# Where the third batch's router logits, its routing and its list entries stand in a gated mixture-of-experts block

## The chip, the core and the metric

The kernel runs on one core of a Trainium2 chip. The metric is the time of one execution in microseconds (us); the kernel before has a median of 522.15 us over 8 runs (516.1 to 529.22). All times on an engine's own clock below count from the start of the profiled span. PE is the matrix engine (PEld its weight loads), DVE the vector engine, ACT the engine for activations, POOL the general engine, SP the engine that here only issues transfers. DMA is the engines that move data.

## What is computed

Four batches of 512 tokens, 512 features each. An attention step adds a mix of features to each token; then a feed-forward step adds a shared expert and, for each token, its two best of eight experts:

```python
x = x + tanh(g_xattn[0]) * xattn(layernorm(x), ctx_1024, Wq, bq, Wk, bk)
x = x + tanh(g_ffn[0])   * ffn(layernorm(x), ...)

def ffn(x, ...):                                  # D = 512, H = 352, E = 8, TOP_K = 2
    shared_out = (silu(x @ Wg_s) * (x @ Wu_s)) @ Wd_s
    logits = x @ Wr + br + rb                     # 8 per token
    probs = sigmoid(logits)
    top_v, top_i = top_k(probs, 2)
    w = one_hot(top_i) * (top_v / sum(top_v))     # per token and expert
    routed_out = sum over e of swiglu(x, Wg[e], Wu[e], Wd[e]) * w[..., e]
    return shared_out + routed_out
```

All matrices are float32.

## The kernel before

**Stages.** B = 4 batches, NS = 4 tiles of 128 tokens in each. First come attention weights and attention output of the batches, with the shared expert's inner layer (`shared_hidden`) of batches 0 and 1 between them. Then, in code after the loop (lines 645 to 663), come the inner layers of batch 2 (`B - 2`, "the third") and batch 3 (`B - 1`, "the last"). After that come the shared expert's outer products of all 16 tiles (`shared_out`), with the search for what each block of the routed part must read between them, and then the routed part: 39 blocks of 128 tokens, each of one expert.

**Inner layer.** `shared_hidden(b, lo, hi, amid)` makes for each tile two products, `pg` (gate) and `pu` (up), each in four steps `c` over the features; `amid[c]` is called after step `c` and puts other small products there. ACT takes silu of `pg` (line 472), DVE multiplies by `pu` (line 475), and ACT's queue writes the tile to `hs_d` for regrouping.

**Logits.** The router's eight columns lie behind the up weights in `ws`. For a batch that isn't in `alone`, `pu` is 360 columns wide instead of 352 and its last eight are the logits (line 474 adds the bias). For a batch in `alone`, `logits(b, lo, hi)` makes them by themselves: for each tile four products of 128x8 (line 443), put amid an inner layer. In the kernel before, `alone` holds batches 2 and 3.

**Input of the inner layer.** The normalised rows of the last batch go to DRAM in quarters (`to_quarters`, POOL's queue, line 321), come back regrouped (`from_quarters`, SP's queue, line 327, `wbig<-xz_d`), and are turned by DVE (`turn`, line 331, `wbig<-wbig`). DVE works in the order of its queue: what stands behind a turn waits for that turn's transfer too.

**Routing.** `route(b)` is a chain of some 25 small DVE steps with one exponential on ACT, which needs another table there (line 497, then line 472's table again). It ends with a running count per expert: `pre` and `cum[b + 1]`, so that batch 3's follows batch 2's. `places(b)` makes two products on PE (line 520, `pl`: `tri` by `sel`, then `ones` by `pre`), from which DVE works out a place in the list for each token and choice (`place`, `ent`, lines 526 to 544). `scatter_places` issues eight scatters on POOL's queue for each batch (line 552, `slot_d<-ent,posi`), each of 128 entries. In the built program POOL's transfers share eight semaphores in turn, so each transfer on POOL's queue waits for the one that stands eight before it to have landed.

**List.** Line 700 (`ws<-slot_d`, POOL's queue) reads the finished list; it waits for all scatters. DVE copies it into another order (line 710, four copies), after the fifth outer product's addition by its place in the queue, and PE multiplies it by `pick` (line 642, `pq`) after the seventh of the 16 outer products (`po`, line 568). From `pq` come the indices of the gathers for the routed blocks.

**Buffers.** The small products and `pg`, `pu` share a pool of four PSUM buffers (`ps_mm`); a product that takes a buffer waits until its last reader is done.

Of the kernel before, what the change touches and what calls it, by code (L numbers as in the profile page):

```python
# [22 lines left out]
def flamingo_block(  # L23
# [17 lines left out]
    B, S, D = x.shape  # L41
# [96 lines left out]
    def after(later, earlier, reason="written before it is read"):  # L138
        tc.add_manual_dep(
            later.ins, earlier.ins.name,  # L140
            mybir.DependencyInfo(mybir.DependencyClass.Sync, mybir.DependencyReason.DATA),
            reason=reason,
        )
# [176 lines left out]
    def to_quarters(src, by, engine=nc.gpsimd):  # L320
        engine.dma_start(
            out=by.rearrange("(a p) w -> p a w", p=P), in_=src.rearrange("p (a w) -> p a w", a=NQ)
        )
# [98 lines left out]
    def normed_turned(b, lo, hi):  # L422
        def turns(behind):
            for s in range(lo, hi):
                t = turn(
                    xn_v[s].rearrange("p (b w) -> p b w", b=NQ), xnT_v[b % 2][:, :, ts(s, P)]
                )
                after(t, behind, "they come in meanwhile")

        return turns  # L430

    lg_b = {}
    alone = {B - 2, B - 1}
    scatters = []

    def logits(b, lo=0, hi=NS):

        if lo == 0:
            lg_b[b] = small.tile([P, NS, E], F32, tag="lg", name=f"lg_{b}")
        pr = ps_mm.tile([P, hi - lo, E], F32, tag="mm", name="pr")  # L440
        for s in range(lo, hi):
            for c in range(ND):
                p = nc.tensor.matmul(
                    pr[:, s - lo, :], lhsT=xnT_v[b % 2][:, c, ts(s, P)], rhs=ws[:, c, 2 * H :],
                    start=(c == 0), stop=(c == ND - 1),
                )
                after(p, product["last"], "not too many small ones at once")
        nc.vector.tensor_tensor(
            lg_b[b][:, lo:hi, :], pr,
            bias_r.rearrange("p (o e) -> p o e", o=1).broadcast_to([P, hi - lo, E]), ALU.add,  # L450
        )

    def shared_hidden(b, lo=0, hi=NS, amid={}):

        route_too = b not in alone
        if route_too and lo == 0:
            lg_b[b] = small.tile([P, NS, E], F32, tag="lg", name=f"lg_{b}")
        wide = HR if route_too else H
        for s in range(lo, hi):
            pg = ps_mm.tile([P, H], F32, tag="mm", name="pg")  # L460
            pu = ps_mm.tile([P, wide], F32, tag="mm", name="pu")
            for c in range(ND):
                for dst, at, n in ((pg, 0, H), (pu, H, wide)):
                    product["last"] = nc.tensor.matmul(  # L464
                        dst, lhsT=xnT_v[b % 2][:, c, ts(s, P)], rhs=ws[:, c, at : at + n],
                        start=(c == 0), stop=(c == ND - 1),
                    )
                if c in amid:
                    amid[c]()
            filled = h_sb[(b * NS + s) % OUT]  # L470
            h = filled[:, :H]
            nc.scalar.activation(h, pg, AF.Silu)
            if route_too:
                nc.vector.tensor_add(lg_b[b][:, s, :], pu[:, H:], bias_r)
            done = nc.vector.tensor_mul(h, h, pu[:, :H])
            at = (b * NS + s) * NQ * P
            to_quarters(filled, hs_d[at : at + NQ * P, :], nc.scalar)
        return done
# [12 lines left out]
    def route(b):  # L491

        lg = lg_b[b]

        nc.vector.tensor_scalar_max(lg, lg, -87.0)
        pr = small.tile([P, NS, E], F32, tag="pr", name=f"pr_{b}")
        nc.scalar.activation(pr, lg, AF.Exp, scale=-1.0)
        nc.vector.tensor_scalar_add(pr, pr, 1.0)
        nc.vector.reciprocal(pr, pr)
        at = [small.tile([P, NS, E], F32, tag=f"at{k}", name=f"at{k}_{b}") for k in range(TOP_K)]  # L500
        m1 = first_max(pr, b, at[0], 0)

        rest = small.tile([P, NS, E], F32, tag="rest", name=f"rest_{b}")
        nc.vector.scalar_tensor_tensor(rest, at[0], -4.0, pr, ALU.mult, ALU.add)
        m2 = first_max(rest, b, at[1], 1)

        sel = small.tile([P, NS, E], F32, tag="sel", name=f"sel_{b}")
        nc.vector.tensor_add(sel, at[0], at[1])
        pre = small.tile([P, NS, E], F32, tag="pre", name=f"pre_{b}")
        nc.vector.tensor_copy(pre[:, 0, :], cum[b])  # L510
        for s in range(NS):
            dst = pre[:, s + 1, :] if s + 1 < NS else cum[b + 1]
            nc.vector.tensor_add(dst, pre[:, s, :], sel[:, s, :])
        return at, m1, m2, sel, pre

    def places(b, at, m1, m2, sel, pre):

        pl = ps_mm.tile([P, NS * E], F32, tag="mm", name="pl")
        for i, (l, r) in enumerate(((tri, sel), (ones, pre))):
            p = nc.tensor.matmul(  # L520
                pl, lhsT=l, rhs=r.rearrange("p s e -> p (s e)"),
                start=(i == 0), stop=(i == 1),
            )
            after(p, product["last"], "the routing takes its time")
        place = small.tile([P, NS, E], F32, tag="place", name=f"place_{b}")
        nc.vector.tensor_add(place, pl.rearrange("p (s e) -> p s e", e=E), first)  # L526
        tot = small.tile([P, NS, 1], F32, tag="tot", name=f"tot_{b}")
        nc.vector.tensor_add(tot, m1, m2)
        nc.vector.reciprocal(tot, tot)
        nc.vector.tensor_scalar_mul(tot, tot, tgf)  # L530
        todo = []
        for k, m in enumerate((m1, m2)):
            nc.vector.tensor_mul(at[k], at[k], place)
            pos = small.tile([P, NS, 1], F32, tag=f"pos{k}", name=f"pos{k}_{b}")
            nc.vector.tensor_reduce(pos, at[k], AX.X, ALU.add)
            posi = small.tile([P, NS], I32, tag=f"posi{k}", name=f"posi{k}_{b}")
            nc.vector.tensor_copy(posi, pos.rearrange("p s o -> p (s o)"))
            low = small.tile([P, NS], I32, tag=f"low{k}", name=f"low{k}_{b}")
            nc.vector.tensor_single_scalar(low, posi, P - 1, op=ALU.bitwise_and)
            ent = small.tile([P, NS, 2], F32, tag=f"ent{k}", name=f"ent{k}_{b}")  # L540
            nc.vector.tensor_tensor(  # L541
                ent[:, :, 0], token[:, b * NS : (b + 1) * NS], low, ALU.subtract
            )
            nc.vector.tensor_mul(
                ent[:, :, 1], m.rearrange("p s o -> p (s o)"), tot.rearrange("p s o -> p (s o)")
            )
            todo += [(ent[:, s, :], posi[:, s : s + 1]) for s in range(NS)]
        return todo

    def scatter_places(todo, behind=None):  # L550
        for what, where in todo:
            sc = nc.gpsimd.indirect_dma_start(  # L552
                out=slot_d, in_=what,
                out_offset=bass.IndirectOffsetOnAxis(ap=where, axis=0),
                in_offset=None,
            )
            tc.declare_no_dep(sc.ins, group="places", reason="no two tokens share a place")
            tc.add_to_no_dep_group("places", sc.ins)
            after(sc, cleared)
            if behind is not None:  # L560
                after(sc, behind, "it delays less there")
            scatters.append(sc)
# [48 lines left out]
    routed = None  # L611
# [4 lines left out]
    for i in range(B):  # L616
# [12 lines left out]
        if i >= 2:  # L629
# [7 lines left out]
            routed = route(i - 2)  # L637
    power, _ = attention_out(B - 1, halves(B - 2))
    scatter_places(places(B - 3, *routed), power)
    def amid(dst, lhsT, rhs):  # L640
# [4 lines left out]
    routed = {}  # L645
    load_expert(4, None, (False, True))
    load_expert(5, None, (True, False))
    shared_hidden(B - 2, 0, 1, {1: lambda: logits(B - 2, 0, 2), 3: lambda: logits(B - 2, 2)})
    routed[B - 2] = route(B - 2)
    step = shared_hidden(B - 2, 1, 2)  # L650
    normed_turned(B - 1, 0, 2)(step)
    load_expert(5, step, (False, True))
    step = shared_hidden(
        B - 2, 2, 3, {1: lambda: scatter_places(places(B - 2, *routed[B - 2]))}
    )
    normed_turned(B - 1, 2, NS)(step)
    step = shared_hidden(
        B - 2, 3, NS, {1: lambda: logits(B - 1, 0, 2), 3: lambda: logits(B - 1, 2)}
    )
    routed[B - 1] = route(B - 1)  # L660
    load_expert(6, step)
    step = shared_hidden(B - 1, 0, 1)
    back_early(step)


# [19 lines left out]
    step = shared_hidden(B - 1, 2, 3, {1: count})  # L685
# [260 lines left out]
```

## Time and profile before

| what | value |
|---|---|
| median of 8 runs | 522.15 us (516.1 to 529.22) |
| profiled execution, time | 517.12 us |
| its span | 513.9 us, so 3.2 us lie around it |
| granted TensorE clock, mean | 0.992 |
| batch 2's inner layers on PE | 134.19 to 162.40 us |
| batch 3's inner layers on PE | 162.40 to 182.88 us |
| outer products, with `pq` and `pi` among them | 182.88 to 222.8 us |
| routed part on PE | 223.69 to 501.9 us |
| a pair of products of one step, `pg` and `pu` | 1.18 us (0.59 us each, start to start) |
| regrouped rows of batch 3: issue to landing | 7.1, 7.5, 6.6 and 9.7 us; issued 144.9 to 149.3 us |
| scatters: landing after issue | 7.3 to 17.3 us, median 10.7 |
| list read, line 700: landing after issue | 5.0 us |
| expert 7's gate and up weights | issued at 183.68 us, landing after 11.0 |

A row of the timeline gives start, duration, engine, line and operation, what is written from what is read, a count, and in brackets the idle time of the engine before it with what ended it. A merged row's duration reaches from its first start to its last end. float32 products are two passes in the trace, so `x2` is one product.

### The profile page before, as it was taken

The page shows a single profiled execution, that of the slowest core. Times are in us where ns is not written, and L with a number is a line of the kernel's source. Part 1 is how long each engine was busy: PE and PEld are TensorE (multiplying, and loading weights), DVE is VectorE, ACT ScalarE, POOL GpSimd, SP SyncE. Part 2 cuts the span into 40 slices and gives each one's busy share as a digit, 9 for nine tenths or more (in the row PEclk, how much of TensorE's full clock was granted, in tenths as well). Part 3 has the DMA queues.
Part 4 walks back from the last instruction along what each step waited for, and adds up shares of the span by engine and source line. Part 5 has one row for each costly group of instructions (what it writes and reads, how often), then busy time and mean ns, then how long its engine had stood idle before and what let it go on. Part 6 is the DMA issues. An engine that isn't in the chain of part 4 may idle for free. (4 is left out here: it accounts for less than half of the span.)

```text
span 513.9 us, 5436 instructions
## 1 busy us (share of the span) xinstructions
PE 493.8 (96%) x1507; PEld 275.2 (54%) x1507; DVE 231.5 (45%) x542; ACT 91.7 (18%) x163; POOL 265.4 (52%) x293
## 2 busy tenths in 40 slices
PE   8999999999999999999999999999999999999980
PEld 4444464465667644455555555555555555555540
DVE  1898965955856356553323322332233333322210
ACT  3355034112022000000111111111111111111110
POOL 3004230171265410545777777777477777777221
PEclk9999999999999999999999999999999999999996
DMA  6999994579998999724666656665555666666332
GB/s 196 395 366 370 340 337 136 163 176 143 314 239 120 215 179 322 219 82 129 123 140 121 124 121 135 124 127 117 122 108 137 128 124 134 123 127 127 55 44 38
DMA packets 67164, 87.86 MB, mean 171 GB/s; under 512 B 32992, under 2 KB 40032, under 8 KB 67136
## 3 DMA queue, kind: packets, MB, share of 16 engines
q1 hardware_dynamic: 43056, 55.08, 36.7%
q0 software_dynamic: 13184, 25.88, 26.8%
q10 hardware_dynamic: 10896, 6.56, 5.6%
q8 instruction: 14, 0.23, 0.2%
q14 instruction: 14, 0.11, 0.1%
HBM read 56.78 MB, written 30.70 MB: 170 GB/s over the span
## 5 line engine op out<-in xcount | busy, mean ns | idle before, releaser
L750 POOL DMA_INDIRECT x_all<-xz_d,idx x148 | 141.7, 957 | 79.8 <-issue 35.4
L331 DVE STREAM_TRANSPOSE x_all<-x_all 128x512 f32<-128x512 f32 (+1 forms) x71 | 69.9, 984 | 160.2 <-DMA x_all<-by 135.9
L785 PE MATMUL rg<-wbig,x_all 128*128 x296 | 111.9, 460 | 1.7 <-issue 0.9
L785 PE MATMUL ru<-wbig,x_all 128*128 x296 | 111.7, 459 | 0.0
L568 PE MATMUL po<-wbig,x_all 128*128 x222 | 101.4, 592 | 0.7 <-DVE x_all L836 0.7
L785 PEld LDWEIGHTS rg<-wbig,x_all 128*128 128x128 f32 x296 | 55.9, 190 | 43.1 <-issue 18.4
L813 POOL DMA_INDIRECT out_x<-ws,idx x37 | 59.6, 1611 | 31.8 <-issue 17.6
L785 PEld LDWEIGHTS ru<-wbig,x_all 128*128 128x128 f32 x296 | 56.2, 190 | 31.3
L568 PEld LDWEIGHTS po<-wbig,x_all 128*128 128x128 f32 x222 | 42.1, 190 | 44.0 <-issue 36.3
L398 PE MATMUL po<-wbig 128*128 128x512 f32 x128 | 56.4, 592 | 0.0
L464 PE MATMUL pu<-ws,wbig 128*128 128x360 f32 (+1 forms) x128 | 48.8, 463 | 1.4 <-DVE place L526 1.4
L464 PE MATMUL pg<-ws,wbig 128*128 128x352 f32 x128 | 49.3, 466 | 0.0
L793 ACT ACTIVATE h_all<-rg 128x352 f32<-128x352 f32 x37 | 17.2, 464 | 173.2 <-PE rg L785 173.2
L317 POOL TENSOR_TENSOR rstd<-ve,mhalf 128x4 f32<-128x4 f32 x8 | 8.2, 1024 | 71.9 <-DVE ve L315 38.5
L812 ACT ACTIVATE ws<-po,wts 128x512 f32<-128x512 f32 x37 | 25.4, 687 | 103.9 <-PE po L568 101.2
L568 PE MATMUL po<-wsd,wqk 128*128 128x512 f32 x96 | 42.5, 595 | 0.3 <-DVE wqk L331 0.3
L552 POOL DMA_INDIRECT slot_d<-ent,posi x32 | 31.1, 971 | 18.6 <-DVE ent L541 9.5
L398 PEld LDWEIGHTS po<-wbig 128*128 128x128 f32 x128 | 24.2, 190 | 29.4 <-issue 27.7
L464 PEld LDWEIGHTS pu<-ws,wbig 128*128 128x128 f32 x128 | 24.2, 190 | 15.3 <-DVE place L526 2.0
L464 PEld LDWEIGHTS pg<-ws,wbig 128*128 128x128 f32 x128 | 23.5, 190 | 12.0 <-issue 0.5
L568 PEld LDWEIGHTS po<-wsd,wqk 128*128 128x128 f32 x96 | 17.9, 190 | 22.0 <-issue 19.6
L331 DVE STREAM_TRANSPOSE wbig<-wbig 128x512 f32<-128x512 f32 x24 | 25.4, 1094 | 6.1 <-DMA wbig<-xz_d 5.7
(135 smaller groups left out, 327.2 us busy)
## 6 DMA issues: line engine op xcount, KB each, us to landing
wbig<-in_Wgu SPq DMA_DIRECT2D x8, 1408.0 KB, 13.7
by<-x_all SPq DMA_DIRECT2D x34, 192.0 KB, 3.2
x_all<-by SPq DMA_DIRECT2D x34, 192.0 KB, 2.4
wbig<-in_Wd SPq DMA_DIRECT2D x8, 768.0 KB, 13.6
x_all<-in_x SPq DMA_DIRECT2D x4, 1024.0 KB, 11.1
wbig<-in_xT SPq DMA_DIRECT2D x4, 1024.0 KB, 10.1
xz_d<-wbig POOLq DMA_DIRECT2D x16, 256.0 KB, 5.3
wbig<-xz_d SPq DMA_DIRECT2D x16, 256.0 KB, 5.3
```

The costliest lines, as they stand in the source:

```text
L317: power = nc.gpsimd.tensor_tensor(rstd, ve, mhalf, ALU.pow)
L331: return nc.vector.transpose(dst.rearrange("p c (j b) -> p b c j", b=NQ), z.rearrange("p b (c i) -> p b c i", i=Q))
L398: product["last"] = nc.tensor.matmul(po, lhsT=xT_v[b % 2][:, c, ts(s, P)], rhs=attT_v[b % 2][:, c, :], start=(c == 0), stop=(c == NN - 1),)
L464: product["last"] = nc.tensor.matmul(dst, lhsT=xnT_v[b % 2][:, c, ts(s, P)], rhs=ws[:, c, at : at + n], start=(c == 0), stop=(c == ND - 1),)
L552: sc = nc.gpsimd.indirect_dma_start(out=slot_d, in_=what, out_offset=bass.IndirectOffsetOnAxis(ap=where, axis=0), in_offset=None,)
L568: product["last"] = nc.tensor.matmul(po, lhsT=hT[:, j, :], rhs=wdj(j), start=(j == 0), stop=(j == NF - 1))
L750: g = nc.gpsimd.indirect_dma_start(out=z[:, q, :], out_offset=None, in_=xz_d, in_offset=at(idx4[:, q, i : i + 1]),)
L785: nc.tensor.matmul(dst, lhsT=xgT[:, c, :], rhs=wbig[:, bass.ds(base[i] + (c * 2 * H + lo), H)], start=(c == 0), stop=(c == ND - 1),)
L793: silu = nc.scalar.activation(sg, pg, AF.Silu)
L812: nc.scalar.activation(y, po, AF.Copy, scale=wts[:, i : i + 1])
L813: nc.gpsimd.indirect_dma_start(out=out, in_=y, out_offset=at(idx[:, i : i + 1]), in_offset=None, compute_op=ALU.add)
```

## The change

Batch 2 leaves `alone`, so its logits come from its widened up products and its two calls of `logits` go. Its routing moves from behind its first tile to behind its fourth, where both batches' routings follow each other (DVE's queue holds them interleaved). Its `places` and eight scatters move from amid its third tile to behind the last step of batch 3's first tile.

```diff
-    alone = {B - 2, B - 1}
+    alone = {B - 1}
...
-    shared_hidden(B - 2, 0, 1, {1: lambda: logits(B - 2, 0, 2), 3: lambda: logits(B - 2, 2)})
-    routed[B - 2] = route(B - 2)
+    shared_hidden(B - 2, 0, 1)
     step = shared_hidden(B - 2, 1, 2)
     normed_turned(B - 1, 0, 2)(step)
     load_expert(5, step, (False, True))
-    step = shared_hidden(
-        B - 2, 2, 3, {1: lambda: scatter_places(places(B - 2, *routed[B - 2]))}
-    )
+    step = shared_hidden(B - 2, 2, 3)
     normed_turned(B - 1, 2, NS)(step)
     step = shared_hidden(
         B - 2, 3, NS, {1: lambda: logits(B - 1, 0, 2), 3: lambda: logits(B - 1, 2)}
     )
-    routed[B - 1] = route(B - 1)
+    for b in (B - 2, B - 1):
+        routed[b] = route(b)
     load_expert(6, step)
-    step = shared_hidden(B - 1, 0, 1)
+    step = shared_hidden(
+        B - 1, 0, 1, {3: lambda: scatter_places(places(B - 2, *routed[B - 2]))}
+    )
     back_early(step)
```

In the built program, PE's queue holds at batch 3's first tiles: the first tile's eight products; `pl<-sel` of batch 2; the first pair of the second tile; `pl<-pre` of batch 2; the second pair; both `pl` of batch 3. SP's queue holds the same transfers in the same order as before. POOL's queue holds the same transfers in the same order too: the 16 scatters of batches 2 and 3, then line 700. DVE's queue has batch 3's turns 0 and 1 ahead of the multiplication of batch 2's third tile, and the first tile of batch 3 is multiplied behind both `sel`.

## The prediction

> **What bounds the kernel now.** I read the busy shares first. PE is at work nearly all the time, so what PE loses or saves counts unless something else takes its place.
>
> ```profile
> PE 493.8 (96%) x1507; PEld 275.2 (54%) x1507; DVE 231.5 (45%) x542; ACT 91.7 (18%) x163; POOL 265.4 (52%) x293
> ```
>
> The chain of waits at the end names only the last scatter and a tail of 1% of the span, so I went on to the timelines of the stage that is edited. On PE, the two sets of logits of batch 2 and the stage's only long wait:
>
> ```profile
> 136.64 1.85 PE L443 MATMUL pr<-ws,wbig 128*128 128x8 f32 x16
> 138.34 0.84 PE L464 MATMUL pg<-ws,wbig 128*128 128x352 f32 x2
> ...
> 140.79 1.85 PE L443 MATMUL pr<-ws,wbig 128*128 128x8 f32 x16
> 142.49 0.84 PE L464 MATMUL pg<-ws,wbig 128*128 128x352 f32 x2
> ...
> 154.66 0.86 PE L464 MATMUL pu<-ws,wbig 128*128 128x352 f32 x2 [1.42 <-DVE place L526]
> ```
>
> A set takes PE from 136.64 to 138.34, which is 1.70 us. The wait of 1.42 us is an up product whose buffer batch 2's places still hold. On DVE, `place` came late because two turns stand ahead of it and wait for rows in flight:
>
> ```profile
> 152.07 1.14 DVE L331 STREAM_TRANSPOSE wbig<-wbig 128x512 f32<-128x512 f32 x1 [3.81 <-DMA wbig<-xz_d]
> 153.51 1.08 DVE L331 STREAM_TRANSPOSE wbig<-wbig 128x512 f32<-128x512 f32 x1 [0.30 <-DMA wbig<-xz_d]
> 154.44 0.17 DVE L526 TENSOR_TENSOR place<-pl,first 128x32 f32<-128x32 f32 x1
> ...
> 158.96 1.11 DVE L331 STREAM_TRANSPOSE wbig<-wbig 128x512 f32<-128x512 f32 x1 [1.61 <-DMA wbig<-xz_d]
> ```
>
> On POOL, the first scatter of batch 2, the first and last of batch 3, and the read of the list:
>
> ```profile
> 155.94 0.96 POOL L552 DMA_INDIRECT slot_d<-ent,posi  x1 [3.58 <-DVE ent L541]
> ...
> 171.67 0.96 POOL L552 DMA_INDIRECT slot_d<-ent,posi  x1 [5.91 <-DVE ent L541]
> ...
> 180.52 0.96 POOL L552 DMA_INDIRECT slot_d<-ent,posi  x1 [0.30 <-issue]
> 191.14 0.59 POOL L700 DMA_DIRECT2D ws<-slot_d  x1 [9.65 <-PE po L568]
> ```
>
> The wait before the read is put down to PE, which had left that product long before. The last scatter landed 9.8 us after its issue, at 190.3, and that is what the read waited for. So eight scatters take eight times (180.52 - 171.67) / 7 = 1.26 us of POOL, and the list lands at 191.14 + 5.0 = 196.1. Its users:
>
> ```profile
> 200.55 0.74 DVE L710 COPY ws<-ws 128x128 f32<-128x128 f32 x4
> ...
> 201.56 0.98 PE L642 MATMUL pq<-pick,ws 128*128 128x39 f32 x8
> ```
>
> From landing to the first `pq` it takes at least one copy (0.26), a weight load (0.19) and their signals; I take 0.85 of the 1.01 between these rows. So `pq` could have begun at 197.0. **The list has 4.6 us to spare, no more.**
>
> **The change part by part.** Sums are made on the profiled execution, 517.12 us, which is 5.0 below the median; the difference found is put on the median.
>
> *PE's work.* Removed: two sets, 2 x 1.70 = 3.4 us, and the wait of 1.42. Added: 16 up products of 360 columns for 352. By columns that is 0.59 x 8/352 = 0.013 each, 0.2 in all; the rows' medians (466 and 459 ns) agree in size. DVE's four additions of 0.16 for two of 0.17, and one pair of ACT table loads fewer (2 x 1.28), lie on engines that are not full there. Alone this would be -4.6 us.
>
> *Where this goes first.* PE would begin the last batch's logits earlier, but their rows come by a chain that the change doesn't touch: normalised rows, POOL's quarters, SP's loads at 144.9 to 149.3, turns at 152.07, 153.51 and 158.96. PE without the two sets reaches the first `pr` at 134.19 + 14 x 1.2 = 151.0, and turns 0 and 1 end at 153.2 and 154.6. The first set ends at 155.5, two pairs follow to 157.9, and the last four products wait for turn 3, which ends at 160.07; they end at 160.9. Before, they ended at 162.40. Of 4.6 us, 1.5 are left here; were the loads earlier, all 4.6 (loads took 6.6 to 9.7 us from issue). I keep 160.9, for its chain is the same.
>
> *The routings.* From the last logits' addition to `sel` the trace shows 162.58 to 166.91 plus 0.18, so 4.5 us, most of it links of 0.225 us in which DVE could take another step each 0.113. Two interleaved chains take some 0.6 more. The exponential's table load began 0.59 ahead of that addition (161.99); now it stands behind the fourth tile's transfer and begins some 0.3 after it, about 0.8 later: `sel` at 160.9 + 0.2 + 5.1 + 0.8 = 167.0. PE wants it for `pl` after the first tile of batch 3, at 160.9 + 4.8 = 165.7, so PE waits some 1.5 us; the pairs behind it in PE's queue wait too. Between 0 (the table is loaded sooner) and 2. At `pn` PE then stands at 173.1, where it stood at 172.40 before. **PE's gain is used up: +0.7 us, -4.6 at best.**
>
> *The scatters.* Batch 2's `place` follows `pl<-pre` behind the next pair, at 169.2; interleaved with the other routing, `ent` takes until 170.5. First scatter 170.8, where batch 3's first stood at 171.67. Bounds: 167.3 (rows in time) and 172. Behind it stand 16 scatters in place of 8: last issue at 170.8 + 15 x 1.264 = 189.8. The ninth must wait for the first to have landed. In the same stretch before, one issued at 171.67 took 12.1 us, against 8 x 1.264 = 10.1 of issuing, so the queue waits 0 to 2.0 longer; the next ones took 11.3 to 9.3, hence I take 1.0: last issue 190.8. Landing: the median 10.7 us. It was 9.8 at the end before, but 13.1 to 14.7 for the scatters issued at 162.3 to 164.8, just behind an expert's weights issued at 161.50; expert 7's are issued at 183.68. Landed 201.5, read 0.8 later as before (190.3 to 191.14), list at 202.3 + 5.0 = 207.3, `pq` at 208.15. **PE wants `pq` at 202.3 and gets it at 208.15.**
>
> Queued behind the read on POOL are the gathers, which need these indices anyway. Behind the copies on DVE stand the outer products' additions, and behind `pq` on PE nine more outer products: all shift together. Nothing after makes it good, since the routed part is PE without gaps of over a microsecond. Against 201.56 that is +6.6 us, whatever PE gained or lost before.
>
> *The clock.* PE would stand still for 5.8 us; its longest wait in the stages before was 1.42. At the end of the trace it does stand still, from 501.85:
>
> ```profile
> 505.00:505.50 0.50, 0.00 (x0) 0.00 (x0) 0.00 (x0) 0.00 (x0) 0.50 (x1) 1.00 0.00 0
> 505.50:506.00 0.50, 0.00 (x0) 0.00 (x0) 0.00 (x0) 0.00 (x0) 0.37 (x1) 0.66 0.00 0
> 506.00:507.00 1.00, 0.00 (x0) 0.00 (x0) 0.00 (x0) 0.00 (x0) 0.00 (x0) 0.50 0.74 57
> ```
>
> The granted clock (third figure from the right) falls to half 3.8 us after the last product. No row shows how long it stays there once work returns. If as long as it took to fall, 3.8 us of matmuls at half speed lose 1.9; if at once, none. I take half: +0.9. [...]
>
> Sum: +6.6 + 0.9 = **+7.5 us**: 524.6 for a profiled execution like this one, **529.7** for the median.
>
> **The rivals.** *The list is early enough.* If the rows of the last batch come sooner, so do routings and scatters, and PE's saving lasts. It decides at the last scatter: issued by 185.1 with a landing of 9.8, PE waits for nothing (180.52 + 4.6). For it speaks that 16 scatters from 167.3 end at 186.3, close to that; against it the untouched chain to the turns. With 186.3 and a landing of 9.8 the list is 1.2 late: +1.2, 523.4. With PE's 1.5 kept and a list in time: 520.7. I take this family from -1.5 to +3.5.
>
> *The full saving.* The same, with PE's 4.6 kept to the end: 517.5. It needs the last scatter at 180.5, so its first at 161.5, when the last batch's logits aren't done; only a much shorter landing helps, and the shortest of 32 is 7.3.
>
> *A long tail.* Expert 7's weights and the returning tiles fill the queues: lane wait 2.0, a landing of 14.7, a list read of 7.9 (the longest of POOL's quarters), the clock's 1.9, first scatter at 171.5. Last issue 192.5, landed 207.2, list 215.9, `pq` 216.75: +15.2 + 1.9 = +17.1 with everything at its worst. Some of these together make +10 to +13, 532 to 535.
>
> *The change doesn't do what it says:* its built queues show it does; only the two `pl` of batch 2 are pulled apart around a pair.
>
> **How the numbers follow.** The list late by 3.5 to 10 us: 0.62, at 529.7. List early: 0.20. Long tail: 0.12. Full saving: 0.06. The range leaves out the full saving, the lower part of the second case and the worst of the third: 522.0 (near no change) to 535.5 (+13.3). Over 1%, which is 5.2 us and about what a measurement here can tell from no change, lie the long tail and nine tenths of the forecast, 0.70; within it the second case, a tenth of the forecast and most of the full saving, 0.26; 4.6 us is itself under 1%, so faster is left with 0.04.
>
> **What would show it.** No `pr` between 134 and 150, and waits of PE for turns near 151 and 158; a wait of 1 to 2 us at `pl<-sel`; 16 scatters in one row from about 171 to 190; line 700 at about 202, where the first copy of line 710 waits for it and not for its turn on DVE; one wait of some 6 us at `pq`, with a granted clock under 1 behind it. I'm wrong if the scatters issue closer than 1.26 us, if line 700 is issued before 195, or if PE waits at `pq` for under 2 us.

## The result, and the profile after

The kernel after has a median of 524.99 us (25 runs, 519.95 to 531.73), beside 519.44 for the kernel before on the same chip (67 runs). The ratio is 1.0096, 95% interval 1.0074 to 1.0118: about 5 us slower. The medians are over all executions (5.55 us apart), while every ratio here leaves out the slow executions, those over 1.5% above the fastest of the same kernel. The profiled execution took 524.2 us, its span is 522.2 (before: 517.12 and 513.9).

The first line of the page of the kernel after, then PE's timeline at the last batch's logits and at tile 5 of the outer products:

```profile
PE 495.2 (95%) x1475; PEld 275.2 (53%) x1475; DVE 228.8 (44%) x544; ACT 88.7 (17%) x161; POOL 264.8 (51%) x293
```

```profile
149.76 0.77 PE L464 MATMUL pu<-ws,wbig 128*128 128x360 f32 x2
155.90 3.55 PE L443 MATMUL pr<-ws,wbig 128*128 128x8 f32 x16 [5.37 <-DVE wbig L331]
159.30 1.52 PE L464 MATMUL pg<-ws,wbig 128*128 128x352 f32 x2
...
164.19 2.33 PE L443 MATMUL pr<-ws,wbig 128*128 128x8 f32 x16
...
187.30 13.04 PE L568 MATMUL po<-wsd,wqk 128*128 128x512 f32 x30
203.17 6.88 PE L568 MATMUL po<-wsd,wqk 128*128 128x512 f32 x12 [2.84 <-DVE wqk L331]
209.89 0.98 PE L642 MATMUL pq<-pick,ws 128*128 128x39 f32 x8
```

PE has 32 instructions fewer and yet is busy 1.4 us longer. It stands still for 5.37 us at the last batch's first `pr` and for 2.84 at tile 5, and what follows runs slowly: a set of `pr` from 155.90 to 159.30 is 3.40 us where it was 1.70, the `pg` behind it takes 1.32 start to start where it took 0.68, twelve passes of `po` 6.88 where they took 5.42. At `pq` PE doesn't wait at all. The same two places before:

```profile
156.54 1.85 PE L443 MATMUL pr<-ws,wbig 128*128 128x8 f32 x16
...
196.30 5.42 PE L568 MATMUL po<-wsd,wqk 128*128 128x512 f32 x12 [0.34 <-DVE wqk L331]
```

DVE's timeline of the kernel after has what PE waited for:

```profile
154.68 2.07 DVE L331 STREAM_TRANSPOSE wbig<-wbig 128x512 f32<-128x512 f32 x2 [10.69 <-DMA wbig<-xz_d]
...
159.16 2.00 DVE L331 STREAM_TRANSPOSE wbig<-wbig 128x512 f32<-128x512 f32 x2 [2.04 <-DMA wbig<-xz_d]
...
202.26 0.85 DVE L331 STREAM_TRANSPOSE wqk<-h_all 128x384 f32<-128x384 f32 x1 [3.71 <-DMA h_all<-hs_d]
...
209.33 0.83 DVE L710 COPY ws<-ws 128x128 f32<-128x128 f32 x4 [0.30 <-DMA ws<-slot_d]
```

The rows of the last batch and the regrouped tile 5 are in flight when DVE is ready for them. The list comes 0.30 us late for DVE and in time for PE. POOL's queue, first and last scatter and the read of the list:

```profile
174.56 0.96 POOL L552 DMA_INDIRECT slot_d<-ent,posi  x1 [21.85 <-DVE ent L544]
...
193.50 0.96 POOL L552 DMA_INDIRECT slot_d<-ent,posi  x1 [0.30 <-DMA slot_d<-ent,posi]
202.85 0.59 POOL L700 DMA_DIRECT2D ws<-slot_d  x1 [8.39 <-DMA h_all<-hs_d]
```

The last scatter landed at 202.05, and tile 5's load, issued at 190.86, at 202.17: they end together. The load took 11.3 us, where it took 8.9 before (186.44 to 195.3). Expert 7's weights, 1408 KB, are in flight beside it in both: they landed at 201.72 after 13.6 us, before at 194.7 after 11.0. The granted clock is the third figure from the right in the windows:

```profile
154.00:155.00 1.00, 0.00 (x0) 0.00 (x0) 0.33 (x1) 0.00 (x0) 0.00 (x0) 0.97 0.28 64
155.00:160.00 5.00, 4.10 (x17) 3.91 (x18) 2.96 (x5) 0.00 (x0) 0.00 (x0) 0.50 0.95 172
160.00:165.00 5.00, 5.00 (x13) 3.17 (x11) 1.74 (x5) 0.46 (x1) 0.00 (x0) 0.50 0.46 100
...
203.00:206.00 3.00, 2.83 (x4) 1.28 (x5) 1.41 (x3) 0.00 (x0) 0.44 (x1) 0.50 0.97 209
```

It is half from 154.94 for 10.24 us, and again from 202.73 for 3.41. The table shows where PE stands in the two executions, in us (starts, but for the first row):

| place on PE | before | predicted | after | after less before |
|---|---|---|---|---|
| last batch's logits end | 162.40 | 160.9 | 166.37 | +3.97 |
| `pn` | 172.40 | 173.1 | 176.82 | +4.42 |
| first outer product | 182.88 | | 187.30 | +4.42 |
| tile 5's product | 196.30 | | 203.17 | +6.87 |
| `pq` | 201.56 | 208.15 | 209.89 | +8.33 |
| routed part | 223.69 | | 232.02 | +8.33 |

The 0.45 between the first two rows is batch 2's two `pl`, which moved here.

### The profile page after: what moved, and what is told of

The parts are those of the page before. It is cut to its first block, busy times and chain, and to the rows that moved or that the text cites. A ratio compares the mean times of both kernels' runs of the same rounds, so it can differ in the third digit from the quotient of the medians.

```text
span 522.2 us, 5379 instructions
## 1 busy us (share of the span) xinstructions
PE 495.2 (95%) x1475; PEld 275.2 (53%) x1475; DVE 228.8 (44%) x544; ACT 88.7 (17%) x161; POOL 264.8 (51%) x293
## 5 line engine op out<-in xcount | busy, mean ns | idle before, releaser
L464 PE MATMUL pg<-ws,wbig 128*128 128x352 f32 x128 | 50.5, 477 | 0.0
L464 PE MATMUL pu<-ws,wbig 128*128 128x360 f32 (+1 forms) x128 | 50.2, 475 | 0.0
L568 PE MATMUL po<-wsd,wqk 128*128 128x512 f32 x96 | 43.9, 611 | 2.8 <-DVE wqk L331 2.8
L331 DVE STREAM_TRANSPOSE wbig<-wbig 128x512 f32<-128x512 f32 x24 | 25.1, 1090 | 13.9 <-DMA wbig<-xz_d 13.6
## 6 DMA issues: line engine op xcount, KB each, us to landing
x_all<-in_x SPq DMA_DIRECT2D x4, 1024.0 KB, 10.7
```

Source lines behind the costliest of these rows:

```text
L331: return nc.vector.transpose(dst.rearrange("p c (j b) -> p b c j", b=NQ), z.rearrange("p b (c i) -> p b c i", i=Q))
L464: product["last"] = nc.tensor.matmul(dst, lhsT=xnT_v[b % 2][:, c, ts(s, P)], rhs=ws[:, c, at : at + n], start=(c == 0), stop=(c == ND - 1),)
L568: product["last"] = nc.tensor.matmul(po, lhsT=hT[:, j, :], rhs=wdj(j), start=(j == 0), stop=(j == NF - 1))
```

## The experiments

The runs came from several chips. Each ratio is to the kernel before on the run's own chip, with its 95% interval; only ratios are compared between chips.

**The change again.** r1, r8 and r13 are the kernel after, unchanged, each on another chip.

> The changed kernel once more, for how much its own waits vary. Theory A (rows and clock: PE, without batch 2's small logits, reaches the last batch's logits before their rows are turned, waits there, and the granted clock halves): again a wait of 3 to 6 us at the first `pr` and a granted clock near 0.5 for some 8 us behind it; +4 to +8 us over the kernel before. Theory B (list: the 16 scatters end late and `pq` waits for the list): `pq` waits for the first copy of line 710 by 2 us or more, in this execution if not in the one seen.

> The changed kernel a third time, on the chip of the three above, for a comparison with the first of them. Theory B: it waits at `pq` or comes there within 1 us of the list, +4 to +8 us over the kernel before; executions with a lower mean clock are the longer ones, by about half of the time at half clock.

> The kernel after, as the common measure of the three runs beside it: 1.010 to 1.015 of the kernel before by the earlier runs. If the two parts add up, its ratio less one is the sum of theirs (r14 and r15).

Measured: 1.0136 (1.0095 to 1.0176), 1.0115 (1.0048 to 1.0181), 1.0102 (1.0035 to 1.0169). The total repeats; the places of the waits don't. PE's waits in r1, then in r8:

```profile
PE pq L642 <- DVE ws L710: 2.9, 1, 2.9
...
PE po L568 <- DVE wqk L331: 1.7, 1, 1.7
```

```profile
PE po L568 <- DVE wqk L331: 4.7, 1, 4.7
PE pr L443 <- DVE wbig L331: 3.2, 1, 3.2
```

In r1 the rows were nearly there (0.24 and 0.48 us of waiting at `pr`) and the list was the last to come: line 700 at 193.08, landed at 201.0, a read of 7.9 us where it took 5.0 before. DVE's first copy then let `pq` begin at 201.42:

```profile
201.09 0.82 DVE L710 COPY ws<-ws 128x128 f32<-128x128 f32 x4 [3.60 <-DMA ws<-slot_d]
```

In r8 PE waits at `pr` and at tile 5, and at `pq` not at all. In r13 it is neither tile 5 nor `pq`, but an outer product far earlier. PE, then ACT, then DVE:

```profile
181.65 0.76 PE L464 MATMUL pu<-ws,wbig 128*128 128x352 f32 x2
182.24 2.74 PE L568 MATMUL po<-wsd,wqk 128*128 128x512 f32 x6
193.69 2.93 PE L568 MATMUL po<-wsd,wqk 128*128 128x512 f32 x3 [8.71 <-DVE wqk L331]
```

```profile
191.44 0.46 ACT L472 ACTIVATE wbig<-pg 128x352 f32<-128x352 f32 x1 [14.21 <-remote]
```

```profile
192.22 0.52 DVE L475 TENSOR_TENSOR wbig<-wbig,pu 128x352 f32<-128x352 f32 x1 [7.60 <-remote]
```

The last inner layer's products ended by 182.4 on PE, and ACT took them up at 191.44, nine microseconds later, with sixteen scatters going out from 169.50 to 188.44. "Remote" means that the trace knows no releaser. A part of the semaphore events is missing from this trace, so I can't say what held ACT. The same wait, 8.6 to 8.7 us, stands in r11 and r12 below.

**The two halves on one chip.** r14 puts batch 2's small logits back and leaves the rest late; r15 takes the small products out of the kernel before and moves nothing. They ran beside r13.

```diff
r14, against the kernel after
-    alone = {B - 1}
+    alone = {B - 2, B - 1}
...
-    shared_hidden(B - 2, 0, 1)
+    shared_hidden(B - 2, 0, 1, {1: lambda: logits(B - 2, 0, 2), 3: lambda: logits(B - 2, 2)})
r15, against the kernel before
-    shared_hidden(B - 2, 0, 1, {1: lambda: logits(B - 2, 0, 2), 3: lambda: logits(B - 2, 2)})
+    shared_hidden(B - 2, 0, 1, {1: lambda: borrowed(0, 2), 3: lambda: borrowed(2, NS)})
```

`borrowed` copies those logits of batch 1 on DVE.

> Undone in the kernel after: batch 2's logits come from sixteen small products each amid its first tile again, as before; its routing, places and scatters stay late. If the late scatters are the cost, 1.007 to 1.012, with the first scatter near 168 us and the last near 187, waits at tile 5 or at pq, and none at pr. If PE's early arrival at pr with a halved clock is the main cost, 1.003 or below, since PE has its small products back and arrives as before.

> Changed in the kernel before: batch 2's 32 small router products are left out and its logits are a copy of batch 1's, so its routing is batch 1's; routing, places and all scatters stand where the kernel before has them. PE has 3.4 us less to do and nothing is moved. If PE's work sets the end, 0.9935; if PE only arrives sooner at rows that aren't there yet, 0.997 to 1.001, with a wait at the last batch's pr of 2 to 3 us; if that wait also halves the clock, 1.000 to 1.006.

Measured: r14 1.0109 (1.0045 to 1.0172), r15 0.9985 (0.9946 to 1.0025), r13 with both 1.0102. On an earlier chip the move alone (r2, the kernel of r14) was 1.0082 (1.0054 to 1.0111) beside 1.0136 for r1:

> Batch 2's logits are made by their small products amid its first tile again (3.4 us of PE); its places and scatters stay late, so 16 scatters still stand in a row. Theory A: PE comes to the last batch's first `pr` some 3.4 us later, waits under 2.5 us there, the granted clock stays at 1.00, and the time is 0 to +3 us against the kernel before. Theory B: the list is as late as in the changed kernel, +5 to +8 us against the kernel before.

So on r13's chip the move costs all of it; on r1's it costs 0.8 of 1.4%, with intervals that overlap. On both, the saved 3.4 us of PE bring no gain that can be told from zero. r14's trace has waits of 0.85 us at `pr`, 2.56 before the second outer product, 0.83 at tile 5 and 0.92 at `pq`. Why the saving brings nothing, PE and DVE of r15 say:

```profile
156.08 1.54 PE L464 MATMUL pu<-ws,wbig 128*128 128x352 f32 x2 [6.17 <-DVE wbig L331]
```

```profile
154.02 1.98 DVE L331 STREAM_TRANSPOSE wbig<-wbig 128x512 f32<-128x512 f32 x2 [8.35 <-DMA wbig<-xz_d]
155.86 0.17 DVE L526 TENSOR_TENSOR place<-pl,first 128x32 f32<-128x32 f32 x1
```

PE comes earlier to the product whose buffer `place` must free; `place` stands behind the turns, and the turns behind the rows. PE waits there until `place` is done at 156.03, for 6.17 us where the kernel before waited 1.42 in its trace, at half clock from about 153.3 to 160.2 (0.83 from 150 to 155, 0.50 to 160, 0.98 to 165). It waits 1.79 us more ahead of the first outer product, where the kernel before didn't wait.

**Eight scatters fewer.** r4 and r9 are the kernel after without batch 2's scatters, r10 is the kernel before without them.

```diff
r4 and r9, against the kernel after
-        B - 1, 0, 1, {3: lambda: scatter_places(places(B - 2, *routed[B - 2]))}
+        B - 1, 0, 1, {3: lambda: places(B - 2, *routed[B - 2])}
```

> The changed kernel without batch 2's eight scatters, so its list entries stay zero and its tokens get no routed part; the rest of the work is the same in size. Theory A: the wait at the first `pr` and the halved clock stay, so at least +3 us remain against the kernel before; the second wait, for the regrouped tile 5 of the outer products, goes if it is the scatters that crowd its transfer, and stays at 2 to 3 us if it isn't. Theory B: the list is early, `pq` waits for nothing, and the time is that of the kernel before within 1.5 us.

> Left out: the eight scatters of batch 2, so its entries in the list stay zero; all else is the kernel after. On another chip this ran at a ratio of 0.994 to the kernel before, with batch 3's scatters at 167 to 176 us. If the change's cost is the late end of sixteen scatters in a row and what they crowd, this is again about 0.994 (0.990 to 0.998), with no wait at pq and none over 2 us at the outer product of tile 5; if the cost is PE's early arrival at the rows of the last batch, those waits at pr stay and the ratio is 1.00 or above.

> Left out: the eight scatters of batch 2, in the kernel before. The control of the run beside it. If batch 2's scatters cost nothing where the kernel before has them (amid batch 2's fourth tile, landing before 176 us), this is 1.000 (0.997 to 1.003), and the gain of the run beside it is PE's saved work alone. If leaving eight scatters out gains by itself, through less crowded transfers, this is 0.994 or below too, and the saving of the widened logits isn't shown.

Measured: r4 0.9937 (0.9915 to 0.996), beside 1.0136 for r1 on the same chip; r9 0.9958 (0.9916 to 1.0001) and r10 0.9958 (0.9918 to 0.9999), on another. PE in r4:

```profile
178.18 18.19 PE L568 MATMUL po<-wsd,wqk 128*128 128x512 f32 x42
196.21 0.98 PE L642 MATMUL pq<-pick,ws 128*128 128x39 f32 x8
```

No wait: the last scatter was issued at 175.86 and line 700 at 184.09. Its routed part begins 5.3 us before r1's (218.32 and 223.63), and r1's waits make that up: 1.68 at tile 5, 2.92 at `pq`, 0.72 at `pr`. (r1's trace is of its fastest execution, so the medians lie further apart.) Tile 5's load, issued at 181.74 in r4 and 181.92 in r1, took 8.0 and 10.2 us. Where batch 2's scatters stand early, leaving them out gains 0.4% (r10); where they stand late, 2.0% (r4 and r1). On r10's chip the kernel after wasn't run as it is, but two versions of it, r11 and r12 below, stand at 1.018 there. r4 and r9 still have batch 2's routing and `places` late, so it is the late scatters themselves that cost. And r10 lowers what r4 seemed to show: with the scatters out of both, no gain of the kernel after over the kernel before is seen (0.9958 each, known to 0.4%).

**Users of the list later.** In r5 (the kernel after) and r6 (the kernel before) the copies, `pq` and `pi` stand two outer products further back.

```diff
-    done = shared_out(1, 0, 2)
+    done = shared_out(1)
...
-    shared_out(1, 2, 3)
+    shared_out(B - 2, 0, 1)
...
-    shared_out(1, 3)
+    shared_out(B - 2, 1, 2)
...
-    shared_out(B - 2)
+    shared_out(B - 2, 2)
```

> The changed kernel with the list's copies, `pq`, the indices and `pi` two outer products (2 x 2.57 us of PE) later in the order; nothing else is moved. Theory B (list: the 16 scatters end late and `pq` waits for the list): the wait at `pq`, 2.9 us in the changed kernel's second execution, is gone, and with it the halved clock behind it; the time falls by 4 to 8 us against the changed kernel and lies 0 to 2 us under the kernel before. Rival C (the scatters crowd the other transfers and it is those that PE waits for, above all the regrouped tile 5): the wait before the sixth outer product stays at 1 to 2 us and the time falls by under 3 us. Theory A (rows and clock): no change beyond 1 us.

> The kernel before with the list used two outer products later. Theory B and rival C: nothing waited there before, so the time stays within 1 us of the kernel before. If it falls by over 2 us, the place of `pq` matters by itself and the reading of the run above falls.

Measured: r5 1.0034 (0.9983 to 1.0086), beside 1.0115 for r8 on the same chip; r6 0.9991 (0.9951 to 1.003). By these ratios the shift takes back 0.8% where the list is late and nothing that shows where it isn't. The intervals of r5 and r8 overlap, and r5's trace has no wait at `pq` but still one at tile 5 (4.29 us), so the split between list and tile 5 isn't settled; that both hang on the late scatters is what r4 shows.

**PE's early arrival.** r3, r11 and r16 add to the kernel after six unused products of 128x512 ahead of the last batch's first `pr`, 5.3 us of PE.

```diff
-        B - 2, 3, NS, {1: lambda: logits(B - 1, 0, 2), 3: lambda: logits(B - 1, 2)}
+        B - 2, 3, NS, {1: lambda: after_busy(6, 0, 2), 3: lambda: logits(B - 1, 2)}
```

> The changed kernel with six products of 128x512 (5.3 us of PE, their result is not used) just ahead of the last batch's first `pr`. Theory A: they stand where PE would wait; the wait at `pr` falls under 1.5 us, the granted clock stays at 1.00 there, and the time falls by 3 to 5 us against the changed kernel although PE does more. Theory B: `pq` waits for the list all the same, the time is the changed kernel's within 1 us; if nothing waits at all, it is 5 us longer.

> Added to the kernel after: six unused products of 128x512, 5.3 us of PE, ahead of the last batch's first pr. If PE stands at that pr for 3 us or more on this chip and its clock is halved behind that, the dead work costs nothing or gains: a ratio to the kernel before of 1.010 or below, no wait over 0.5 us at pr and a granted clock of 1.00 between 155 and 165 us. If rows are in time here, PE has no gap to fill, and the dead work moves up the arrival at the list, where it is waited for: again near 1.012. If PE's own work sets the end, 5.3 us more: 1.020 or above.

> Added to the kernel after: six unused products of 128x512, 5.3 us of PE, ahead of the last batch's first pr. Beside r13 on the same chip: if the dead products only fill a gap that PE has anyway, within 0.3% of r13; if the gap is small here, the 5.3 us are waited for less at the list and tile 5, and up to 0.3% more; if they bring on late signals at the last inner layer, as in one earlier run, 0.6% or more above r13, and r13 shows no such signals.

Measured: 1.0128 (1.0102 to 1.0154) beside 1.0136 of r1; 1.0184 (1.0154 to 1.0215), with no kernel after beside it; 1.0105 (1.0047 to 1.0163) beside 1.0102 of r13. On two chips 5.3 us of dead work cost under 0.1%, each ratio known to 0.3 to 0.7%: they fall into time that PE stands still or waits for later. In r3 the waits at `pr` are gone, with 1.31 us left at tile 5 and 2.11 at `pq`. In r11 PE waits nowhere at `pr`, with a clock of 1.00, and then 8.74 us at the second outer product, as in r13.

r12 holds the writes of batch 2's first two tiles back, to see whether they delay the rows; r7 is the kernel before with batch 2's `place` ahead of the first two turns.

```diff
r12, against the kernel after
-            to_quarters(filled, hs_d[at : at + NQ * P, :], nc.scalar)
+            if (b, s) in late:
+                held.append((filled, at))
+            else:
+                to_quarters(filled, hs_d[at : at + NQ * P, :], nc.scalar)
...
+    for filled, at in held:
+        to_quarters(filled, hs_d[at : at + NQ * P, :], nc.scalar)
r7, against the kernel before
-    normed_turned(B - 1, 0, 2)(step)
...
+    normed_turned(B - 1, 0, 2)(placed[B - 2])
```

> Changed in the kernel after: the writes to hs_d of batch 2's first two tiles, which stand at 141 and 144 us beside the last batch's rows, wait until its fourth tile is issued. If those writes are what delays the rows (9 us from issue to landing against 7 before), the rows land some 2 us sooner, PE waits under 2 us at pr, and the ratio to the kernel before is 1.007 or below. If rows are late for another reason, or the time is set at the list and tile 5, it is as the change itself, 1.010 to 1.014; later tiles could also make the load for tile 0 of the outer products late, which would show as a wait at the first po.

> The kernel before with the last batch's first two turns put behind batch 2's `place` on DVE, by a dependency. The wait of 1.42 us of an up product for `place` should be gone, batch 2's scatters begin 3 to 5 us sooner, and nothing else gets later, since the turns wait for their rows until after that anyway: 1 to 1.5 us under the kernel before. If PE then waits for the rows instead, under 0.5 us is gained.

Measured: r12 1.0178 (1.0099 to 1.0256), with 2.4 us of waiting at `pr` and 8.6 at an outer product; r7 0.9988 (0.9946 to 1.003). r12 is no better than the change, and r7 can't be told from the kernel before: the 1 to 1.5 us expected of it lie inside its interval. r12 doesn't clear the writes of blame, since it also has the wait of 8.6 us that r13 has, which hides what the writes are worth; why rows take 7 us in one execution and 9 in the next stays open. No version beat the kernel before with all its work in it.

## Why the prediction was right or wrong

**Right: slower, and by the late scatters.** It is slower by 0.96%, just under the 1% to whose far side the prediction gave 0.70 (its parts, 0.12 and nine tenths of 0.62, make 0.68). Sixteen in a row at 1.26 us, first at 174.56 for 170.8 and last at 193.50 for 190.8, line 700 at 202.85 for 202.3, `pq` at 209.89 for 208.15. That these come so close is partly luck: the row began 3.8 us late, but no wait for a semaphore lengthened it (0 for 1.0), and the last scatter landed after 8.55 us for 10.7. In the other runs of this kernel the first stands at 165.62, 169.95 and 169.50. r4, r10 and r14 show that their lateness is the cost.

**Right: PE's saving is used up before `pn`.** r15, which has the saving without the move, agrees: 3.4 us less work bring 0.15%, with 0.54% as the most that its interval allows. But how it goes was mis-sized. The wait at the first `pr` was put at 2.2 us (151.0 to 153.2), by a chain "that the change doesn't touch"; it was 5.37, since the first rows landed 9.3 us after issue, where they had taken 7.1. In r1 it was 0.24. The wait of 1.5 at `pl<-sel` didn't come (0.20 in r8): the sum had 6.1 us from the end of the logits to `sel`, and the first `sel` was done after 4.2, 4.9 and 5.0 (after, r1, r8). The exponential's table load began 0.2 to 1.0 us ahead of the last logits' addition in these traces, not behind it.

**Wrong: the wait behind the term of +6.6 at the list.** The step that failed is "PE wants `pq` at 202.3 and gets it at 208.15", with the list as the one thing that PE waits for. Measured at `pq`: no wait after, in r8 and in r13, 0.92 in r14, 1.21 in r2, 2.92 in r1; the prediction itself named a wait under 2 us there as a sign of being wrong. The list came about when the sum said, but PE came to `pq` at 209.89, not 202.3, since it had waited 5.37 at `pr` and 2.84 at tile 5, with half the clock behind each. Tile 5's load is issued (190.86) just ahead of the last three scatters and lands with the last, and PE waits for that first: 2.84 us after, 1.68 in r1, 4.73 in r8, none in r4. The prediction let other transfers delay the scatters (its long tail), but not the scatters delay another transfer that PE needs. How they do it stays open: in five traces (before, after, r1, r4, r8) tile 5's load lands 0.5 to 0.9 us behind expert 7's weights, and these too came sooner with eight scatters fewer, after 9.8 us in r4 and 12.4 in r1. Here the waits in a row didn't add up: behind the 5.37 us at `pr` and the 2.84 at tile 5, none was left at `pq`.

How much the list would cost by itself can still be read. In r1, where PE waited for it, `pq` began 0.33 us after the start of the first copy (201.09 and 201.42). After, that copy began at 209.33, so with the scatters where they stood `pq` couldn't have begun before about 209.66, 8.1 us behind the kernel before, even if PE had waited nowhere ahead of it. In this execution the list and the waits ahead of it end within 0.3 us of each other. So a tile 5 that came sooner would by itself have gained at most those 0.3 us; without the eight late scatters both waits go (r4).

**Wrong: the clock, +0.9 with bounds of 0 and 1.9.** In the profiled execution half clock cost 1.70 on the first `pr` set, 2.44 on two pairs (4.89 for 2.45) and 0.48 on the second set, 4.62 in all, and 1.46 on the twelve passes of `po`. The bounds assumed one stand-still, at `pq`, and that the clock comes back at the latest in the 3.8 us that it took to fall; at the logits it took 10.24.

**The sum.** 7.5 us against 5.5 between the medians; the two profiled executions differ by 7.1 in time and 8.3 in span. Counted as waits of PE, the terms traded places: list 0 for 6.6, tile 5 2.50 for none (2.84 less the 0.34 of before), clock 6.1 for 0.9. With the saving of 4.6, the wait of 5.37 and a stage begun 0.66 earlier, they add up to 8.7, 0.4 over the 8.3 measured. Most of that is the saving, which was nearer 5.1: from the start of batch 2's inner layers to the first `pr` PE took 22.35 us before (134.19 to 156.54), 0.44 of it the two `pl` that moved, and 16.8 after without the wait (133.53 to 150.35). The base was off as well: 522.15 was the median of 8 runs, 519.44 that of 67. So 529.7 was 4.7 too high, 2.7 of it from the base, and the range of 522.0 to 535.5 holds 524.99.

**The rivals.** The full saving (0.9% of the time) lies outside r15's interval. The list in time with part of the saving kept (520.7) is what r4 seemed to be until r10 took it back. The long tail has its list read of 7.9 us in r1, yet not its total.

## What to carry to other kernels

Work taken off the busiest engine brought nothing here (r15: 0.9985), ahead of a transfer that didn't come sooner: look for the next wait on data, and run the saving alone before paying for it with a reordering. When many small transfers are moved later, follow every transfer that is issued among them, not only the one that needs them. Test a suspected cost in the kernel before too: all that the kernel after gained on it without eight scatters, it gained itself without them (0.9958 each, r9 and r10). And where PE doesn't wait, look how close the next thing that it needs came: the list here was 0.3 us from being the wait.

## What the runs showed of the hardware

**The halved stretches of the clock had lengths near 3.41, 6.83 and 10.24 us.** After, the clock records have two halved stretches ahead of the kernel's end, of 10.24 and 3.41 us: three times 3.41, and once. In r9 two last 3.41 each. Added up from the mean clock of windows of 2 to 20 us, other runs have stretches of 3.4 to 3.5 us (r3, r5, r6, r8, r13, r14), 6.8 to 6.9 (r5, r8, r12, r13, r14, r15) and 10.2 (r11). What sets the length was not shown. At tile 5 it was 3.41, with a wait of 2.84 (6.8 in r8, with a wait of 4.73). At the last batch's logits it was 10.24, from 154.94: PE resumed at 155.90 and was at work all through the last 6.83. And in r9 windows cut at the steps of the clock read:

```profile
152.15:155.56 3.41, 2.40 (x18) 2.23 (x19) 1.96 (x4) 0.00 (x0) 0.52 (x1) 1.00 1.13 53
155.56:158.97 3.41, 3.41 (x8) 1.88 (x6) 1.09 (x1) 0.36 (x1) 0.00 (x0) 0.50 0.72 62
158.97:162.39 3.42, 2.45 (x19) 2.25 (x18) 1.63 (x5) 0.39 (x2) 0.00 (x0) 1.00 0.83 275
162.39:165.80 3.41, 3.41 (x7) 1.94 (x7) 2.44 (x20) 2.63 (x4) 0.00 (x0) 0.50 0.77 123
```

Windows with PE busy 70 and 72%, most of it 128x8 products, are each followed by a halved one; the longest wait ahead of them is 1.51 us. In r6 a halved stretch of 3.5 us follows 3.41 us with PE busy 91% (158.5 to 161.9), 1.9 us of it such products. After, the second 3.41 us from 154.94 hold 0.95 us of them, and the third, the last at half clock, 0.99. Whether the small products bear on the clock was not tested by itself.

**Small scatters and other transfers.** Between 186 and 195 us, with the last scatters on their way, the kernel after moved 94 GB/s; before, with the last scatter landed at 190.3, it was 261, and 1408 KB of weights were on their way in both. On two chips, sixteen in a row went with signals that ACT and DVE took up 8 to 10 us late (r11, r12, r13); eight in the same place, on one of these chips, did not (r9: ACT 0.6 us behind the product), nor did sixteen in the traces after, r1 and r8 (under 0.1 us). What holds the signals stays open.
